# Four z columns of half B computed with half A's bank in a gated recurrence (one core)

## The chip, the cores and the metric

The kernel runs on one core of a Trainium2 chip. A core has TensorE (matrix products into PSUM), VectorE (called DVE in the profile), ScalarE (ACT), GpSimd (POOL) and SyncE (SP, which issues the transfers). Each engine works through its own queue in order; they meet through semaphores, on which an instruction waits. The metric is the device time of one execution in microseconds. Three executions of the kernel before gave 1624.98, 1625.23 and 1625.85 us, and their median is 1625.23 us.

## What is computed

A recurrence over 512 time steps, batch 8, width 512, all in fp32, and a residual:

```python
def step(h, x_t):
    fused = sigmoid(concatenate([x_t, h]) @ w_W + w_b)
    hidden_state, output_state = split(fused, 2)        # r and z
    memory_state = x_t @ wx_W + wx_b + hidden_state * (h @ wh_W + wh_b)
    h_new = output_state * h + (1.0 - output_state) * tanh(memory_state)
    return h_new, h_new
out = x + all h_new                                     # h starts from cond_1024
```

Below r is `hidden_state` and z is `output_state`. The products with x do not depend on the state and can be made ahead. The three products with h (512 x 512 each, for r, z and wh) are on the way from each step to the next.

## The kernel before

**Layout.** The 512 units of the state are four blocks of 128. A block's units 0 to 63 belong to half A, units 64 to 127 to half B. A product has 32 rows of batch (four steps of 8, of which one step's are live) and is written to one of four row strips of a PSUM bank, strip `j` (rows 32j to 32j+31) for block `j`. The sum over the 512 old units is split into four chunks `k`: chunks 0 and 1 come from half A of the old state, 2 and 3 from half B. So "A0" is the products of chunk 0 into bank A, four strips side by side, and fp32 makes two passes of each.

**Banks.** Three banks take the products of a step, in two sets that alternate from group to group of four steps (`banks`, line 215). Bank A (256 columns) holds half B's part of wh for chunks 0 and 1, then half A's wh, z and r. Bank D (128 columns) holds half B's z and r. Bank H (64 columns) holds half B's wh for chunks 2 and 3. Before a group begins ScalarE copies the group's x products, with the biases, into the banks (`spread`, line 310, from `xs`); the columns of x for the memory state go through VectorE (`turn_x`). `XP` (line 73) says which columns of `xs` go where.

**Order of a step.** `tc.manual_schedule()` (line 213) keeps the order of each queue as it is written. TensorE takes A0 A1 A2 A3 D0 D1 D2 D3 H2 H3 (`ORDER`, line 27) and then some pieces of the x products (`deal`, lines 555 to 558): three pieces in most steps, four in each sixteenth. In the last 17 steps no x products are left. A2 and A3 leave out bank A's first 64 columns. A0 and A1 need the new half A of the state, A2 and A3 its half B.

After the products VectorE transposes 32 x 32 blocks, because gates and state live with units on partitions. The steps of the element work stand in lines 656 to 688, in this order:

- `turn_r(0)`, `turn_h(0)`, `turn_r(1)`, `turn_z()`: half A's r, wh and z out of bank A (L585, L594, L577), each followed by its sigmoid on ScalarE (line 285 is the helper that records all of ScalarE's activations).
- `memory(0, 0)`: for chunk 0 a scan on VectorE (L565) forms r times wh plus x, and a tanh on ScalarE follows.
- `turn_part()` (L638): half B's part of wh out of bank A. It is the last read of bank A in a step.
- `memory(0, 1)`: the same scan and tanh for chunk 1.
- `turn_r_b()` (L577 and two sigmoids): half B's r out of bank D. Behind them on ScalarE stands `sz`, the sigmoid of half B's 64 z columns, taken straight from bank D.
- `update(0, 0)`, `turn_h(1)` (L594 out of bank H), `update(0, 1)`: the scans that write half A's new state, with bank H's transpose between them.
- `memory(1, 0)`, `memory(1, 1)`: half B's scans and tanhs.
- `turn_sz` (L631): half B's z, after its sigmoid, is transposed from `sz`.
- `update(1, 0)`, `update(1, 1)`: half B's new state.

Small memsets of a tile `idle` stand at some places (`settle`, `turn_sz`); they take a wait ahead of the instruction behind them. `act` (line 284) also removes a dependence between two activations that write the same place. All other waits are set by the framework from what each instruction reads and writes.

Of the kernel before, what the change touches and what calls it, by code (L numbers as in the profile page):

```python
# [7 lines left out]
F32 = mybir.dt.float32  # L8
BF16 = mybir.dt.bfloat16
AF = mybir.ActivationFunctionType  # L10
# [3 lines left out]
P = 128  # L14
NQ = 4
GS = 4
B = 8
HU = 64
# [9 lines left out]

FIRST = "A0 A1 x A2 x x A3 H0 H1 H2 H3 x D0 D1 D2 D3"

BANKS = {"A": 256, "D": 128, "H": 64}

HALF = 192

# [35 lines left out]

SC = slice(128, 512)

XP = {"A": slice(0, 256), "X": slice(256, 384), "D": slice(384, 512), "H": slice(512, 576)}


@with_exitstack
def tile_cond_rnn_residual(
# [43 lines left out]
    const = ctx.enter_context(tc.tile_pool(name="const", bufs=1))  # L121
    xin_p = ctx.enter_context(tc.tile_pool(name="xin", bufs=4))
    out_p = ctx.enter_context(tc.tile_pool(name="outp", bufs=3))
    work = ctx.enter_context(tc.tile_pool(name="work", bufs=4))
# [11 lines left out]
    def load_x(c, half=slice(0, 2), ks=slice(0, NQ)):  # L136

        if c < NCH:
            if c not in xins:
                xins[c] = xin_p.tile([P, 2, NQ, TC * B // 2], F32, tag="xin", name=f"xin_{c}")  # L140
            nc.sync.dma_start(
                out=xins[c][:, half, ks],
                in_=x[c].rearrange("p (e k n) -> p e k n", e=2, k=NQ)[:, half, ks],
            )
# [13 lines left out]
        if k == 0:  # L158
            load_x(0, 1)

    wa = const.tile([P, NQ, NQ, 256], F32, name="wa")
    for k in range(NQ):
        nc.sync.dma_start(out=wa[:, k], in_=wa_d[k])
        if k == 0:
            load_x(1, slice(0, 1))
    wd = const.tile([P, NQ, NQ, 128], F32, name="wd")
    nc.sync.dma_start(out=wd[:, :3], in_=wd_d)
    nc.sync.dma_start(out=wd[:, 3], in_=wd3_d)
    load_x(1, slice(1, 2))
# [38 lines left out]
    def state(hf, i, slot=2):  # L208

        s = i % GS  # L210
        return hT[hf][i % NH][:, B * s : B * s + B, :, slot]

    ctx.enter_context(tc.manual_schedule())
    whole = [{n: psum.tile([P, 512], F32, name=f"{n}{q}") for n in BANKS} for q in range(2)]
    banks = [{n: whole[q][n][:, :w] for n, w in BANKS.items()} for q in range(2)]
    xps = [psum.tile([P, 512], F32, name=f"xp{q}") for q in range(2)]

    def mm(out_, lhsT, rhs, start=False):
        nc.tensor.matmul(  # L219
            out_, lhsT, rhs, start=start, stop=False, skip_group_check=True  # L220
        )
# [62 lines left out]
    def act(key, out_, in_, func, **kw):  # L284
        inst = nc.scalar.activation(out_, in_, func, **kw).ins  # L285
        if key in written:
            tc.declare_no_dep(inst, written[key], reason="ordered through VectorE")
        written[key] = inst
        return inst
# [12 lines left out]
    def keep(g):  # L302

        nc.scalar.copy(xs[g % GS][:, SC], bank_of(g)[:, COLS])

    def source(g, c0, c1):

        return xs[g % GS][:, c0:c1] if g else xps[0][:, c0 - 64 : c1 - 64]

    def spread(g, names):  # L310

        for n in names:
            skip = 64 if n == "A" and not g else 0
            nc.scalar.copy(banks[g % 2][n][:, skip:], source(g, XP[n].start + skip, XP[n].stop))

    def turn_x(g, e):

        c0 = XP["X"].start + 32 * e
        nc.vector.transpose(md1[e // 2][g % 2][:, :, e % 2, 1 + e // 2], source(g, c0, c0 + 32))
# [10 lines left out]
    def inner_weight(n, p, j=slice(0, 2)):  # L330

        a, b = [
            (block(p, 0, 1, j), block(p, 0, 0, j)),
            (block(p, 1, 1, j), ti[:, p, 0, j]),
            (block(p, 1, 1, j), block(p, 0, 1, j)),
            (block(p, 1, 0, j), ti[:, p, 1, j]),
        ][n]
        nc.vector.tensor_tensor(ti[:, p, n, j], a, b, ALU.subtract)
# [113 lines left out]
    def take(it, n=None):  # L452
        while n is None or n > 0:
            if next(it, it) is it:
                return
            n = None if n is None else n - 1

    def x_side():
        for c in range(2, NCH):
            yield from products(c)  # L460
# [9 lines left out]
    later = x_side()  # L470
# [53 lines left out]
    for i in range(T):  # L524
        g, s = divmod(i, GS)
        c, t = divmod(i, TC)
        ps = banks[g % 2]
# [7 lines left out]
        for n in (ORDER if i else FIRST).split():  # L535
            if n == "x":
                take(first[1], 1)
                if k_ == 0:
                    keep(2)
                k_ += 1  # L540
                continue
            bank, k = n[0], int(n[1])
            hs = hT[k // 2][i % NH][:, :, k % 2, 2]
            to, w_ = {
                "A": (ps["A"], wa) if k < 2 else (ps["A"][:, 64:], wa[:, :, :, 64:]),
                "D": (ps["D"], wd),
                "H": (ps["H"], wa[:, :, :, :64]),
            }[bank]
            if bank == "A" and i == 0:
                to, w_ = xps[0][:, :HALF], wa[:, :, :, 64:]  # L550
            for j in range(NQ):
                mm(to[32 * j : 32 * j + 32, :], hs, w_[:, k, j])
        if i == 0:
# [9 lines left out]
        def scan(c_, out_, d0, d1):  # L563

            return nc.vector.tensor_tensor_scan(  # L565
                *[t_[:, :, c_].rearrange("p n c s -> p (n c s)") for t_ in (out_, d0, d1)],
                0.0,
                ALU.mult,
                ALU.add,
            ).ins  # L570

        pa = ps["A"][:, HU:] if i else xps[0][:, :HALF]
        raw = {"h": (pa[:, :HU], ps["H"]), "z": (pa[:, HU : 2 * HU],), "r": (pa[:, 2 * HU :], ps["D"][:, HU:])}

        def turned(n, hf):
            t_ = work.tile([P, 2, 32], F32, tag=f"t{n}{hf}", name=f"t{n}{hf}_{i}")
            inst = nc.vector.transpose(t_.rearrange("p c n -> p (c n)"), raw[n][hf]).ins  # L577
            return t_[:, :, rows], inst
# [5 lines left out]
        def turn_r(q):  # L584
            nc.vector.transpose(tr[:, q], raw["r"][0][:, 32 * q : 32 * q + 32])  # L585
            act(
                ("r", 0, q, g % 2, s),
                md0[0][g % 2][:, rows, q : q + 1, 1].rearrange("p n c -> p c n"),
                tr[:, q : q + 1, rows],
                AF.Sigmoid,  # L590
            )

        def turn_h(hf):
            inst = nc.vector.transpose(  # L594
                md1[hf][g % 2][:, :, :, hf].rearrange("p n c -> p c n"), raw["h"][hf]
            ).ins
            h_done[hf] = inst
            if hf == 0 and i + 1 - NH in pool_done:
                tc.add_manual_dep(inst, pool_done[i + 1 - NH].name, SYNC)
# [16 lines left out]
        def turn_r_b():  # L616
            t_, _ = turned("r", 1)
            for q in range(2):
                act(
                    ("r", 1, q, g % 2, s),  # L620
                    md0[1][g % 2][:, rows, q : q + 1, 2].rearrange("p n c -> p c n"),
                    t_[:, q : q + 1],
                    AF.Sigmoid,
                )
            sz = work.tile([P, HU], F32, tag="sz", name=f"sz_{i}")
            act(("sz", i % 4), sz, ps["D"][:, :HU], AF.Sigmoid, scale=-1.0)
            return sz

        def turn_sz(sz):
            done = [  # L630
                nc.vector.transpose(hd0[1][i % 2][:, :, q, 2], sz[:, 32 * q : 32 * q + 32]).ins  # L631
                for q in range(2)
            ]
            mark = nc.vector.memset(idle[:, IDLE - 3 : IDLE - 2], 0.0).ins
            tc.add_manual_dep(mark, done[0].name, SYNC)

        def turn_part():
            nc.vector.transpose(md1[1][g % 2][:, :, :, 0].rearrange("p n c -> p c n"), ps["A"][:, :HU])  # L638
# [6 lines left out]
        def memory(hf, q):  # L645

            c_ = slice(q, q + 1)
            scan(c_, ms[hf], md0[hf][g % 2][:, rows], md1[hf][g % 2][:, rows])
            act(("n", hf, q, i % NH), state(hf, i, 1)[:, :, c_], ms[hf][:, :, c_, 1 + hf], AF.Tanh)

        def update(hf, q):
            new = hT[hf][(i + 1) % NH][:, B * s1 : B * s1 + B]
            z_ = hd0[hf][i % 2][:, rows] if hf else hd0[hf][i % 2]
            return scan(slice(q, q + 1), new, z_, hT[hf][i % NH][:, rows])

        turn_r(0)
        turn_h(0)
        turn_r(1)
# [1 line left out]
        memory(0, 0)  # L660
        if i:
            turn_part()
        memory(0, 1)
        if i == 0:
            for p in (3, 4):
                inner_weight(0, p)
        sz = turn_r_b()
        update(0, 0)
        turn_h(1)
        update(0, 1)  # L670
# [5 lines left out]
        if i == T - 1:  # L676
# [4 lines left out]
                ALU.add,  # L681
            )
        memory(1, 1)
        turn_sz(sz)
        update(1, 0)
        update(1, 1)
        for hf in range(2):
# [130 lines left out]
```

## Time and profile before

| | us |
|---|---|
| median of three runs | 1625.23 |
| the profiled execution | 1626.4 |
| its span (first to last instruction) | 1624.6 |
| TensorE busy | 1613.8 (99%) |
| weight loads busy | 1311.1 (81%) |
| VectorE busy | 1414.4 (87%) |
| ScalarE busy | 1092.7 (67%) |
| GpSimd busy | 539.7 (33%) |

The durations come from one profiled execution, 1.2 us above the median. In the profile PE stands for TensorE's products, and PEld for its weight loads, which run beside the products; `hT` is the state, `md0` and `md1` feed the scans for the memory state, `hd0` holds z for the scans that write the new state, `tr` and `tz` are transposed products, `m` is the memory state, `xp` the banks of the x products. A row of the time line gives start, length, engine, line, operation, tiles (written <- read), shape and count; neighbouring instructions of a kind are merged into one row. In brackets stands how long the engine was idle before it and what ended that. Matmuls are pipelined and their ends are modelled, so a busy share of 99% doesn't say that the products run at their full rate: the starts of the sets of products do.

### The profile page before, as it was taken

How to read it: one execution, taken by the hardware profiler on the slowest of the kernel's cores; microseconds unless marked ns; L12 is line 12 of the kernel's file. 1: busy time of each engine (PE TensorE's matmuls, PEld its weight loads, DVE VectorE, ACT ScalarE, POOL GpSimd, SP SyncE). 2: the span in 40 equal slices, each digit the busy share in tenths (PEclk: the TensorE clock that was granted, in tenths of full speed). 3: DMA queues.
4: the chain of work that ended last, by engine and by line, in shares of the span. 5: the costliest groups of instructions: out<-in, count | busy, mean ns of one | idle time of the engine just before them, and what ended most of it. 6: DMA issues, size and time to landing. Idle time of an engine off the chain costs nothing.

```text
span 1624.6 us, 121051 instructions
## 1 busy us (share of the span) xinstructions
PE 1613.8 (99%) x49211; PEld 1311.1 (81%) x49211; DVE 1414.4 (87%) x12269; ACT 1092.7 (67%) x6545; POOL 539.7 (33%) x1443
## 2 busy tenths in 40 slices
PE   9999999999999999999999999999999999999998
PEld 6888888888888888888888888888888888888876
DVE  8988888888888888888888888888888888888887
ACT  4766666666666666666666666666666666666666
POOL 2223333333333333333333333333333333333321
PEclk9999999999999999999999999999999999999999
DMA  5011111111111111111111111111111111111110
GB/s 192 12 40 33 29 37 38 43 32 31 33 42 40 35 33 32 39 39 38 35 29 37 38 43 32 30 34 42 40 34 35 31 39 38 38 35 24 31 35 10
DMA packets 66225, 62.10 MB, mean 38 GB/s; under 512 B 9856, under 2 KB 64000, under 8 KB 65664
## 3 DMA queue, kind: packets, MB, share of 16 engines
q1 hardware_dynamic: 65664, 54.35, 12.8%
q8 instruction: 385, 6.31, 1.6%
q14 instruction: 176, 1.44, 0.3%
HBM read 14.96 MB, written 8.39 MB: 14 GB/s over the span
## 4 chain that ended last, share of the span: by engine, by line
PE 98%; DVE 1%; DMA 0%; issue 0%; SPq 0%; ACT 0%
PE A L219 49%; PE D L219 27%; PE xp L219 16%; PE H L219 7%; DMA wx<-in_wx_dram 0%; DVE tr L585 0%; DVE md1B L638 0%; DVE tr L577 0%; DVE md1A L594 0%; DVE tz L577 0%; DVE hT L565 0%; DVE m L565 0%; SPq L132 0%; ACT hT L285 0%; DVE hd0B L631 0%
## 5 line engine op out<-in xcount | busy, mean ns | idle before, releaser
L219 PE MATMUL A<-wa,hT 128*32 128x256 f32 x16352 | 875.8, 354 | 3.8 <-DVE hT L565 3.8
L219 PEld LDWEIGHTS A<-wa,hT 128*32 128x32 f32 x16352 | 500.5, 123 | 256.5 <-DVE hT L565 132.9
L219 PE MATMUL D<-wd,hT 128*32 128x128 f32 x16384 | 541.1, 273 | 0.0
L219 PEld LDWEIGHTS D<-wd,hT 128*32 128x32 f32 x16384 | 480.7, 122 | 21.4 <-issue 0.3
L734 POOL TENSOR_TENSOR ot<-xin,hT 128x32 f32<-128x32 f32 x503 | 135.1, 269 | 1043.1 <-DVE hT L565 1025.5
L285 ACT ACTIVATE md0A<-tr 128x8 f32<-128x8 f32 x1024 | 215.7, 211 | 375.9 <-DVE tr L585 366.9
L285 ACT ACTIVATE hT<-m 128x8 f32<-128x8 f32 x2048 | 380.7, 210 | 46.1 <-DVE m L565 0.2
L585 DVE STREAM_TRANSPOSE tr<-A 128x32 f32<-128x32 f32 x1022 | 199.6, 195 | 198.8 <-PE A L219 197.8
L285 ACT ACTIVATE hT<-hT 128x16 f32<-128x16 f32 x1024 | 232.1, 227 | 92.5 <-DVE hT L565 91.1
L219 PE MATMUL H<-wa,hT 128*32 128x64 f32 x8208 | 208.4, 219 | 0.0
L219 PEld LDWEIGHTS H<-wa,hT 128*32 128x32 f32 x8208 | 185.8, 122 | 0.0
L565 DVE TENSOR_TENSOR_SCAN hT<-hd0B,hT 128x24 f32<-128x24 f32 x1024 | 172.0, 208 | 1.4 <-DVE hT L565 1.4
L565 DVE TENSOR_TENSOR_SCAN m<-md0A,md1A 128x16 f32<-128x16 f32 x1024 | 172.0, 168 | 0.0
L565 DVE TENSOR_TENSOR_SCAN hT<-hd0A,hT 128x24 f32<-128x24 f32 x1024 | 169.5, 166 | 0.0
L285 ACT ACTIVATE md0B<-tr 128x8 f32<-128x8 f32 x1024 | 159.9, 206 | 1.1 <-DVE tr L577 1.1
L565 DVE TENSOR_TENSOR_SCAN m<-md0B,md1B 128x24 f32<-128x24 f32 x1024 | 154.5, 192 | 0.0
L631 DVE STREAM_TRANSPOSE hd0B<-sz 128x32 f32<-128x32 f32 x1024 | 148.9, 190 | 0.0
L219 PE MATMUL xp<-ti,si 128*32 128x192 f32 (+1 forms) x3120 | 146.8, 295 | 0.0
L450 POOL TENSOR_TENSOR xs<-ff 128x192 f32<-128x192 f32 x240 | 139.8, 599 | 0.1
L638 DVE STREAM_TRANSPOSE md1B<-A 128x64 f32<-128x64 f32 x511 | 133.1, 260 | 0.0
L577 DVE STREAM_TRANSPOSE tr<-D 128x64 f32<-128x64 f32 x512 | 127.8, 250 | 0.1
L594 DVE STREAM_TRANSPOSE md1B<-H 128x64 f32<-128x64 f32 x512 | 127.3, 249 | 0.0
(110 smaller groups left out, 1855.6 us busy)
## 6 DMA issues: line engine op xcount, KB each, us to landing
ff<-tt SPq DMA_DIRECT2D x120, 96.0 KB, 2.4
ff<-tt SPq DMA_DIRECT2D x120, 72.0 KB, 2.5
out_dram<-ot SPq DMA_DIRECT2D x128, 64.0 KB, 1.8
xin<-in_x_dram SPq DMA_DIRECT2D x112, 64.0 KB, 2.1
ff<-ff SPq DMA_DIRECT2D x60, 96.0 KB, 2.1
ff<-ff SPq DMA_DIRECT2D x60, 72.0 KB, 2.7
wx<-in_wx_dram SPq DMA_DIRECT2D x4, 768.0 KB, 8.3
wa<-in_wa_dram SPq DMA_DIRECT2D x4, 512.0 KB, 10.6
```

What stands on the lines that cost most here:

```text
L219: nc.tensor.matmul(out_, lhsT, rhs, start=start, stop=False, skip_group_check=True)
L285: inst = nc.scalar.activation(out_, in_, func, **kw).ins
L450: nc.gpsimd.tensor_tensor(to, a, b, ALU.add)
L565: return nc.vector.tensor_tensor_scan(*[t_[:, :, c_].rearrange("p n c s -> p (n c s)") for t_ in (out_, d0, d1)], 0.0, ALU.mult, ALU.add,).ins
L577: inst = nc.vector.transpose(t_.rearrange("p c n -> p (c n)"), raw[n][hf]).ins
L585: nc.vector.transpose(tr[:, q], raw["r"][0][:, 32 * q : 32 * q + 32])
L594: inst = nc.vector.transpose(md1[hf][g % 2][:, :, :, hf].rearrange("p n c -> p c n"), raw["h"][hf]).ins
L631: nc.vector.transpose(hd0[1][i % 2][:, :, q, 2], sz[:, 32 * q : 32 * q + 32]).ins
L638: nc.vector.transpose(md1[1][g % 2][:, :, :, 0].rearrange("p n c -> p c n"), ps["A"][:, :HU])
L734: pool_done[i + 1] = nc.gpsimd.tensor_tensor(ot[:, t], x_of(c, slice(0, NQ), t, 1), hTs[(i + 1) % NH][:, :, :, B * s1 : B * s1 + B, 2].rea ...
```

## The change

Four of half B's z columns (units 64 to 67 of each block) leave bank D and are appended to bank A. Bank A becomes 260 columns wide (196 in A2 and A3), bank D 124. The weights `wa` and `wd`, the biases, the x columns and the copies into the banks follow. The sigmoid `sz` is split in two: the 60 later columns stay where they were, behind half B's r. The four early ones are read from bank A by an activation of their own, which stands on ScalarE behind the tanh of `memory(0, 0)` and ahead of that of `memory(0, 1)`; in the program's order it follows `turn_part`. Both write one tile `sz`, which is transposed as before.

```diff
+EARLY = 4
+
-BANKS = {"A": 256, "D": 128, "H": 64}
+BANKS = {"A": 256 + EARLY, "D": 128 - EARLY, "H": 64}
...
-XP = {"A": slice(0, 256), "X": slice(256, 384), "D": slice(384, 512), "H": slice(512, 576)}
+XP = {
+    "A": slice(0, 256 + EARLY),
+    "X": slice(256 + EARLY, 384 + EARLY),
+    "D": slice(384 + EARLY, 512),
+    "H": slice(512, 576),
+}
...
-    wa = const.tile([P, NQ, NQ, 256], F32, name="wa")
+    wa = const.tile([P, NQ, NQ, BANKS["A"]], F32, name="wa")
...
-    wd = const.tile([P, NQ, NQ, 128], F32, name="wd")
+    wd = const.tile([P, NQ, NQ, BANKS["D"]], F32, name="wd")
...
-                to, w_ = xps[0][:, :HALF], wa[:, :, :, 64:]
+                to, w_ = xps[0][:, : HALF + EARLY], wa[:, :, :, 64:]
...
-        pa = ps["A"][:, HU:] if i else xps[0][:, :HALF]
-        raw = {"h": (pa[:, :HU], ps["H"]), "z": (pa[:, HU : 2 * HU],), "r": (pa[:, 2 * HU :], ps["D"][:, HU:])}
+        pa = ps["A"][:, HU:] if i else xps[0][:, : HALF + EARLY]
+        raw = {
+            "h": (pa[:, :HU], ps["H"]),
+            "z": (pa[:, HU : 2 * HU],),
+            "r": (pa[:, 2 * HU : 3 * HU], ps["D"][:, HU - EARLY :]),
+        }
...
-            sz = work.tile([P, HU], F32, tag="sz", name=f"sz_{i}")
-            act(("sz", i % 4), sz, ps["D"][:, :HU], AF.Sigmoid, scale=-1.0)
-            return sz
-
-        def turn_sz(sz):
+            act(("sz", i % 4), sz[:, EARLY:], ps["D"][:, : HU - EARLY], AF.Sigmoid, scale=-1.0)
+
+        def turn_sz():
...
+        sz = work.tile([P, HU], F32, tag="sz", name=f"sz_{i}")
         turn_r(0)
...
         memory(0, 0)
         if i:
             turn_part()
+        act(("sz early", i % 4), sz[:, :EARLY], pa[:, 3 * HU :], AF.Sigmoid, scale=-1.0)
         memory(0, 1)
...
-        sz = turn_r_b()
+        turn_r_b()
...
-        turn_sz(sz)
+        turn_sz()
```

On the host the columns of the weights and biases are put in the new order (`early` is units 64 to 67 of a block, `later` units 68 to 127):

```diff
+    early, later = slice(64, 64 + EARLY), slice(64 + EARLY, 128)
...
-    wa_d = chunks(cat((whm, half_b), (whm, half_a), (z[D:], half_a), (r[D:], half_a)))
-    wd = units(cat((z[D:], half_b), (r[D:], half_b)))
+    wa_d = chunks(cat((whm, half_b), (whm, half_a), (z[D:], half_a), (r[D:], half_a), (z[D:], early)))
+    wd = units(cat((z[D:], later), (r[D:], half_b)))
```

More of the change, by code (lines that the diff above doesn't have):

```diff
@@ L785, in chunks @@
         return c_(units(a).swapaxes(0, 1))
-    wx_d = chunks(cat((z[:D], half_a), (r[:D], half_a), (wxm, both), (z[:D], half_b), (r[:D], half_b)))
-    wa_d = chunks(cat((whm, half_b), (whm, half_a), (z[D:], half_a), (r[D:], half_a)))
-    wd = units(cat((z[D:], half_b), (r[D:], half_b)))
+    wx_d = chunks(
+        cat((z[:D], half_a), (r[:D], half_a), (z[:D], early), (wxm, both), (z[:D], later), (r[:D], half_b))
+    )
+    wa_d = chunks(cat((whm, half_b), (whm, half_a), (z[D:], half_a), (r[D:], half_a), (z[D:], early)))
+    wd = units(cat((z[D:], later), (r[D:], half_b)))
     wd_d, wd3_d = c_(wd[:, :3]), c_(wd[:, 3])
@@ L792 @@
     bias_d = (
-        cat((whb, half_a), (zb, half_a), (rb, half_a), (wxb, both), (zb, half_b), (rb, half_b), (whb, half_b))[0]
+        cat(
+            (whb, half_a),
+            (zb, half_a),
+            (rb, half_a),
+            (zb, early),
+            (wxb, both),
+            (zb, later),
+            (rb, half_b),
+            (whb, half_b),
+        )[0]
     )
```

## The prediction

> **What bounds it now.** I read the cores' spans first, then the chain that ended last, then one step of the time line, then the last steps. The clock was never throttled:
>
> ```profile
> core 0: 1624.6 us, clock 1.000
> ```
>
> In the chain every piece of a step in the middle of the run is TensorE's (start us, length us, what):
>
> ```profile
> 799.84 1.52 PE A L219 x32
> 801.37 0.87 PE D L219 x32
> 802.24 0.22 PE H L219 x16
> 802.46 0.49 PE xp L219 x16
> 802.95 1.53 PE A L219 x32
> ```
>
> A step takes 802.95 - 799.84 = 3.11 us. Bank D's products stream 4 x 128 columns in 0.87 us, 1.70 ns for a column of all four row strips. Bank A's 2 x 256 + 2 x 192 = 896 columns would take 1.523 at that rate; the row shows 1.53 at its widest. So TensorE alone needs about 3.10 us, and some 0.01 us of a step is lost inside bank A. Where? The same step, all engines:
>
> ```profile
> 801.18 1.06 PE L219 MATMUL D<-wd,hT 128*32 128x128 f32 x32
> 801.43 0.22 DVE L585 STREAM_TRANSPOSE tr<-A 128x32 f32<-128x32 f32 x1 [0.50 <-PE A L219]
> ...
> 802.04 0.26 DVE L638 STREAM_TRANSPOSE md1B<-A 128x64 f32<-128x64 f32 x1
> ...
> 802.16 0.43 ACT L285 ACTIVATE hT<-m 128x8 f32<-128x8 f32 x2
> 802.20 0.15 DVE L565 TENSOR_TENSOR_SCAN m<-md0A,md1A 128x16 f32<-128x16 f32 x1
> ...
> 802.31 0.25 DVE L577 STREAM_TRANSPOSE tr<-D 128x64 f32<-128x64 f32 x1
> 802.48 0.17 DVE L565 TENSOR_TENSOR_SCAN hT<-hd0A,hT 128x24 f32<-128x24 f32 x1
> ...
> 802.59 0.31 ACT L285 ACTIVATE md0B<-tr 128x8 f32<-128x8 f32 x2
> ...
> 802.77 1.71 PE L219 MATMUL A<-wa,hT 128*32 128x256 f32 x32
> ...
> 802.86 0.20 DVE L565 TENSOR_TENSOR_SCAN m<-md0B,md1B 128x24 f32<-128x24 f32 x1
> ...
> 803.09 0.32 ACT L285 ACTIVATE hT<-m 128x8 f32<-128x8 f32 x2
> ...
> 803.34 0.33 DVE L565 TENSOR_TENSOR_SCAN hT<-hd0B,hT 128x24 f32<-128x24 f32 x2
> ...
> 803.60 0.51 PEld L219 LDWEIGHTS A<-wa,hT 128*32 128x32 f32 x16 [0.26 <-DVE hT L565]
> ...
> 804.30 1.06 PE L219 MATMUL D<-wd,hT 128*32 128x128 f32 x32
> ```
>
> There are two loops. Half A: bank A ends, half A's scans (802.48) give A0 and A1 their weights for 802.77. Half B: bank D ends, is transposed (802.31), takes sigmoid (802.59), scan (802.86), tanh (803.09) and scan (803.34), and A2's weights load at 803.60. A0 and A1 end at 802.77 + 512 x 1.70 ns = 803.64, and a load stands about 0.04 us ahead of its product (estimate from the last steps, below). So A2 is ready a hair late: this is the lost 0.01 us. TensorE and half B's loop are nearly level.
>
> Does half B's loop start with bank D, or with VectorE's queue? Bank D's last products end 0.87 us after bank A's, by the chain; VectorE's first read of A starts at 801.43, and 801.43 + 0.87 = 802.30, where the read of D starts (802.31). VectorE itself would have been free some 0.04 us earlier: where a transpose follows a scan at once, it starts about 0.07 before the scan's end, and this scan ends at 802.35. So the start follows bank D.
>
> In the last steps, which have no x products, TensorE itself waits:
>
> ```profile
> 1571.32 0.62 PEld L219 LDWEIGHTS A<-wa,hT 128*32 128x32 f32 x16 [0.39 <-DVE hT L565]
> 1571.32 1.77 PE L219 MATMUL A<-wa,hT 128*32 128x256 f32 x32 [0.24 <-DVE hT L565]
> ...
> 1572.91 1.06 PE L219 MATMUL D<-wd,hT 128*32 128x128 f32 x32
> ...
> 1574.42 0.44 PE L219 MATMUL A<-wa,hT 128*32 128x256 f32 x4 [0.24 <-DVE hT L565]
> ```
>
> They take 3.10 us all the same: half B's loop. From A's first load to D's first product are 1.59 us against 1.53 in the middle (802.77 to 804.30). Of the 0.06, I give 0.04 to the time from a load to its product and the rest to half B.
>
> **The change, part by part.** *Columns.* Bank A gains 4 columns in each of four k, bank D loses as many: 16 x 1.70 = 27 ns added, 27 removed. No product is added. TensorE's own need stays 3.10 us. That 260, 196 and 124 columns run at the same rate is not shown (every width in the trace is a multiple of 32); between exact and rounded up to the next 8 (A +32 columns, D +0, 54 ns a step) I take exact, because the widths 64, 128 and 896 all give 1.70 to 1.72.
>
> *Half B's loop.* Bank D ends 27 ns earlier after bank A, and its transpose can follow (VectorE is free 40 ns earlier). A2 and A3 get 14 ns longer. The loop loses 13 ns and meets TensorE's 3.10: worth at most the lost 0.01 us in each of some 490 steps, 5 to 7 us.
>
> *Half A's loop.* It loses cover: D is 27 ns shorter, so A0 is due at 802.743 instead of 802.77. Its scan also moves 27 ns forward, being queued behind the transpose of D: end 802.65 becomes 802.62.
>
> *The small sigmoid on ScalarE.* 128 x 4, once a step. The nearest rows are the 64-column sigmoid of D (0.20) and the 8-column ones:
>
> ```profile
> L285 ACT ACTIVATE md0A<-tr 128x8 f32<-128x8 f32 x1024 | 215.7, 211 | 375.9 <-DVE tr L585 366.9
> ...
> L285 ACT ACTIVATE sz<-D 128x64 f32<-128x64 f32 x512 | 104.4, 204 | 0.0
> ```
>
> ```profile
> 16.54 0.32 ACT L314 COPY A<-xp 128x192 f32<-128x192 f32 x1
> ...
> 16.89 0.32 DVE L319 STREAM_TRANSPOSE md1A<-xp 128x32 f32<-128x32 f32 x2 [0.69 <-ACT A L314]
> ```
>
> I take 0.15 to 0.21 us, and 0.06 to 0.11 until the next can start (a pair of some 0.21 each takes 0.31 at the least, at 802.59). When does it start? The last two rows show the program holding VectorE's read of a PSUM bank until ScalarE's read of the same bank ends (16.86, then 16.89), though neither writes there. So the sigmoid must wait for the transpose L638 that ends at 802.30 and, in an instruction of its own, for TensorE. Half A's second tanh, queued behind it, goes from 802.38 (the pair at 802.16 ends at 802.59, less 0.21) to about 802.42 to 802.50. Behind that tanh wait the second half-A scan and bank D's sigmoids (due 27 ns earlier than before, at 802.565, and 0.10 to 0.12 behind the tanh): between nothing and 0.05 us late. I take 0.01 us, as most of the interval meets the due time. The 64-column sigmoid becomes 60 wide: nothing.
>
> The Trainium skill, page "ScalarE: Activation LUTs", section "What ACT_TABLE_LOAD costs", gives an activation with immediates 186 ns + 0.833 ns a column, with 93 ns of overlap; its 239 ns for 64 columns is not what the trace shows (204). By the page the small one takes 189 ns and blocks for about 96, which stays inside what I allow.
>
> *A0's wait.* Bank A now has a reader on ScalarE. The next step's A0, which writes the bank, must wait for VectorE (weights) and for ScalarE. The sigmoid itself is done by about 802.6, no matter. But a second wait is a second instruction: the queues of VectorE and ScalarE show such waiting instructions of their own (515 and 128), and TensorE shows once what one costs when it ends last. Only one state tile is cleared by GpSimd, that of step 7, so there A2's load waits for two engines:
>
> ```profile
> L565 DVEq EVENT_SEMAPHORE  x515: 21/21/21, 23.0 to 1621.7; - x172
> ```
>
> ```profile
> L285 ACTq EVENT_SEMAPHORE  x128: 17/17/17, 36.0 to 1620.9; - x128
> ```
>
> ```profile
> 0.73 0.30 POOL L191 MEMSET hT<- 128x192 f32 x1 [0.29 <-POOLq L802]
> ...
> 43.16 0.21 DVE L565 TENSOR_TENSOR_SCAN hT<-hd0B,hT 128x24 f32<-128x24 f32 x1
> ...
> 43.48 0.17 PEld L219 LDWEIGHTS A<-wa,hT 128*32 128x32 f32 x4
> ...
> 802.70 0.14 PEld L219 LDWEIGHTS A<-wa,hT 128*32 128x32 f32 x4
> ```
>
> With one wait the load starts 0.05 us after the scan's end (802.65, 802.70), and the four strips' loads start within 0.02 (0.14 less one load's 0.12). With two it starts 0.11 after (43.37, 43.48), and the last strip 0.05 after the first. The 43.48 load had an old GpSimd wait beside a fresh VectorE wait, just what A0 gets, with ScalarE's the old one. So A0's first load comes at 802.62 + 0.11 = 802.735 (exact ends), its product at 802.775, 0.03 us after it is due; the last strip lags 0.03 more. Behind A0 stands everything of the step. What queues on TensorE behind A0 is A1 to A3 and D, and VectorE waits for their last strip.
>
> It concerns steps whose bank was read in the step before: three of each group of four (the groups take turns with two sets of banks). From a level start they cost, against 3.113 now (the 3.11 above, a digit finer): the first +19 ns (3.10 + 0.03), the second and third +49 each (the lag of 0.03 is met by VectorE, which sees bank A end that much later, and made anew). The fourth has no double wait: it pays the lag back through half B's loop, 3.10 + 0.03 against 3.113, +17. Together 134 ns in four steps. Every sixteenth step has a fourth x piece, 0.16 us of cover, so one of its +49 is hidden:
>
> ```profile
> 1565.20 1.53 PE A L219 x32
> 1566.72 0.87 PE D L219 x32
> 1567.82 0.65 PE xp L219 x16
> 1568.47 1.56 PE A L219 x32
> ```
>
> Sum: 32 x (4 x 134 - 49) = 15.6 us, with 128 x 0.01 = 1.3 us for ScalarE's delay in the fourth steps: about +16 us. The bounds of A0's wait are nothing (the old wait moves to the extra instruction, and VectorE's stays at the load) and 62 ns a step with the lag. I take the step-7 row, as it is the only one with both waits on TensorE.
>
> The rest I cost at nothing: 512 more ScalarE instructions and copies of 260 and 124 columns in place of 256 and 128 lie beside ScalarE's wait for the next bank A (0.7 us a step, the 366.9 us of the md0A row); uncovered, four columns of a copy are 0.007 us, by the 192 columns in 0.32. Bank A's weights grow by 32 KB and bank D's shrink as much; the transfers lie under the first x products, and uncovered they are 0.2 us, once, at the first slice's rate:
>
> ```profile
> GB/s 192 12 40 33 29 37 38 43 32 31 33 42 40 35 33 32 39 39 38 35 29 37 38 43 32 30 34 42 40 34 35 31 39 38 38 35 24 31 35 10
> ```
>
> No queue of SyncE or GpSimd is touched.
>
> The profiled execution took 1626.4 us, 1.8 over its span of 1624.6; the median of the runs is 1625.23. 1626.4 + 16 = 1642.4, so **1641 us** on the median's scale.
>
> The Trainium skill, page "PSUM — Partial Sum Buffer", section "PSUM bank collisions raise a hardware error", says that two engines must be kept apart on one bank and quadrant, reads against reads included; the pair at 16.89 agrees. By that rule both new waits are needed, and the time is the one above; were reads free, ScalarE's delay alone (1.3 us) would go.
>
> **Rivals.** (a) *A0's double wait costs nothing*, because the late wait stays on the load. For it: A0 had 0.03 us to spare (802.70 + 0.04 against 802.77). Against it: step 7. Then the loop's 13 ns is won: 12 ns x 490 = 5.5 us, **1619.7**, if ScalarE's delay stays under 0.013; this is the case on the other side. Chance 0.20. (b) *The wait comes, but in part*: the lag of the strips or the late load alone. 0 to 19 ns in three steps of four, less 13 in the fourth: **1623 to 1632**, middle 1629. Chance 0.16. (c) *The forecast*, 1634 to 1648. Chance 0.55. (d) *The transpose of D does not move*, VectorE's queue holding it: A0's load is 27 ns later still in some 350 steps, +9 us, **1650**; chance 0.05. (e) *The new widths run rounded up*: 54 ns a step, 27 us, **1652** or more; chance 0.04.
>
> **How the numbers follow.** Forecast 1641. The range 1618 to 1650 takes in (a), (b), (c) with its bounds and the near half of (d); the rest of (d), (e) and the far ends of (a) and (c) stay outside, under 2 in 10. About 0.2% (3.2 us) is what a measurement of this kernel can tell from no change: faster is (a) less 0.01, 0.19; same is 0.07 of (b) and that 0.01, 0.08; slower is 0.09 of (b) with (c), (d) and (e), 0.73.
>
> **What would show it.** Right: in three steps of four A0's first load starts 0.11 us after half A's scan and TensorE shows idle time ahead of A0; the chain passes through VectorE and A0's load; steps of 3.13 to 3.16 us. The transpose of D starts 0.85 us, not 0.88, after VectorE's first read of A. A2's load no longer ends a wait that matters. Wrong: steps of 3.10 us with A0's loads at 0.05 us after the scan (rival a); D's sigmoids over 0.05 us late behind the second tanh would make ScalarE the place instead.

## The result and the profile after

The changed kernel takes 1642.7 us in the median (1641.5 to 1642.9), the kernel before beside it 1625.85 (1625.0 to 1626.4): a ratio of 1.0102 (1.0087 to 1.0117), 16.9 us more. The profiled execution took 1642.7 us too, its span 1640.8, again with the clock at 1.000.

The chain that ended last, in the middle of the run (start us, length us, what):

```profile
801.03 1.59 PE A L226 x32
802.62 0.85 PE D L226 x32
...
804.18 1.54 PE A L226 x32
...
807.28 1.60 PE A L226 x32
```

Bank D takes what it should (0.85 us is the 0.87 of before less 27 ns). The loss lies in bank A: 1.59 and 1.60 us in two of these steps, 1.54 in the one between. Two steps of the time line, the lines of the path alone, the step without loss first:

```profile
802.67 0.22 DVE L596 STREAM_TRANSPOSE tr<-A 128x32 f32<-128x32 f32 x1 [0.62 <-PE A L226]
...
803.41 0.21 ACT L292 ACTIVATE hT<-m 128x8 f32<-128x8 f32 x1
...
803.52 0.25 DVE L588 STREAM_TRANSPOSE tr<-D 128x64 f32<-128x64 f32 x1
...
803.64 0.17 ACT L292 ACTIVATE sz<-A 128x4 f32<-128x4 f32 x1
803.69 0.17 DVE L572 TENSOR_TENSOR_SCAN hT<-hd0A,hT 128x24 f32<-128x24 f32 x1
803.71 0.21 ACT L292 ACTIVATE hT<-m 128x8 f32<-128x8 f32 x1
...
803.91 0.66 PEld L226 LDWEIGHTS A<-wa,hT 128*32 128x32 f32 x16
...
806.40 0.26 DVE L647 STREAM_TRANSPOSE md1B<-A 128x64 f32<-128x64 f32 x1
806.52 0.21 ACT L292 ACTIVATE hT<-m 128x8 f32<-128x8 f32 x1
...
806.78 0.17 ACT L292 ACTIVATE sz<-A 128x4 f32<-128x4 f32 x1
806.81 0.17 DVE L572 TENSOR_TENSOR_SCAN hT<-hd0A,hT 128x24 f32<-128x24 f32 x1
806.85 0.20 ACT L292 ACTIVATE hT<-m 128x8 f32<-128x8 f32 x1
...
807.08 0.21 DVE L572 TENSOR_TENSOR_SCAN hT<-hd0A,hT 128x24 f32<-128x24 f32 x1
807.09 0.65 PEld L226 LDWEIGHTS A<-wa,hT 128*32 128x32 f32 x16 [0.19 <-ACT hT L292]
```

Half A's first scan, which writes A0's weights, ends at 803.69 + 0.17 = 803.86, and A0's load starts at 803.91: 0.05 us. In the next step it ends at 806.98 and the load starts at 807.09: 0.11 us. That the row names ScalarE (`<-ACT hT`) doesn't mean that ScalarE was late: what A0 waits for there is the early sigmoid, and that ended at 806.95 (806.78 + 0.17), before the scan. The profile names the engine of the wait that the load itself holds, and the last thing which that engine had done (here a tanh that A0 does not wait for). VectorE's wait, which ended last, sits in a waiting instruction ahead of the load that the time line does not show. The trace has it: in three steps of four, those whose bank was read by the early sigmoid, an event instruction (one that only waits) on TensorE's queue waits for VectorE, and the load behind it holds ScalarE's semaphore alone (378 of 383 such loads). Over the run these loads stand 0.114 us after the scan (median), the others 0.052.

On ScalarE the extra instructions can be counted (row of events: count, shortest/median/longest, first and last start):

```profile
L292 ACTq EVENT_SEMAPHORE  x637: 17/17/38, 26.0 to 1636.8; - x160
```

There were 128 of them before. The early sigmoid starts at 806.78, 0.12 us after the read of the bank that it must wait for (806.40 + 0.26); in the step before, 0.09 us after it (803.29 + 0.26, 803.64). Here too the trace has VectorE's wait in the extra instruction.

### The profile page after: what moved, and what is told of

The parts are those of the page before. It is cut to its first block, busy times and chain, and to the rows that moved or that the text cites. A ratio compares the mean times of both kernels' runs of the same rounds, so it can differ in the third digit from the quotient of the medians.

```text
span 1640.8 us, 122576 instructions
## 1 busy us (share of the span) xinstructions
PE 1630.6 (99%) x49211; PEld 1399.0 (85%) x49211; DVE 1411.8 (86%) x12269; ACT 1070.3 (65%) x7057; POOL 538.5 (33%) x1443
## 4 chain that ended last, share of the span: by engine, by line
PE 98%; DVE 1%; ACT 0%; issue 0%; ACTq 0%
PE A L226 50%; PE D L226 26%; PE xp L226 16%; PE H L226 7%; DVE tr L596 0%; DVE md1B L647 0%; ACT md0A L292 0%; ACT hT L292 0%; ACT sz L292 0%; DVE md1A L605 0%; DVE tz L588 0%; DVE tr L588 0%; DVE m L572 0%; ACT hd0A L292 0%; DVE hT L572 0%
## 5 line engine op out<-in xcount | busy, mean ns | idle before, releaser
L226 PE MATMUL A<-wa,hT 128*32 128x260 f32 x16352 | 903.5, 359 | 4.8 <-ACT hT L292 2.6
L226 PEld LDWEIGHTS A<-wa,hT 128*32 128x32 f32 x16352 | 562.7, 123 | 213.2 <-DVE hT L572 111.2
L226 PE MATMUL D<-wd,hT 128*32 128x124 f32 x16384 | 538.8, 269 | 0.0
L226 PEld LDWEIGHTS D<-wd,hT 128*32 128x32 f32 x16384 | 489.9, 122 | 7.6 <-issue 0.3
L292 ACT ACTIVATE hT<-m 128x8 f32<-128x8 f32 x2048 | 376.3, 208 | 50.5
L226 PE MATMUL H<-wa,hT 128*32 128x64 f32 x8208 | 219.9, 219 | 0.0
L226 PEld LDWEIGHTS H<-wa,hT 128*32 128x32 f32 x8208 | 195.8, 122 | 0.0
L572 DVE TENSOR_TENSOR_SCAN hT<-hd0A,hT 128x24 f32<-128x24 f32 x1024 | 191.4, 187 | 1.8 <-ACT hT L292 1.8
L292 ACT ACTIVATE md0B<-tr 128x8 f32<-128x8 f32 x1024 | 156.6, 203 | 1.4 <-DVE tr L588 1.1
L226 PE MATMUL xp<-ti,si 128*32 128x192 f32 (+1 forms) x3120 | 152.1, 295 | 0.0
```

The costliest lines, as they stand in the source:

```text
L226: nc.tensor.matmul(out_, lhsT, rhs, start=start, stop=False, skip_group_check=True)
L572: return nc.vector.tensor_tensor_scan(*[t_[:, :, c_].rearrange("p n c s -> p (n c s)") for t_ in (out_, d0, d1)], 0.0, ALU.mult, ALU.add,).ins
```

## The experiments

Seven kernels were run, each beside the kernel before. Three ask which part of the change is the loss, one tries a way round it, and three ask what it is about two waits that costs.

### The wait alone

The kernel before; A0 gets the second wait and nothing else changes.

```diff
-                mm(to[32 * j : 32 * j + 32, :], hs, w_[:, k, j])
+                inst = mm(to[32 * j : 32 * j + 32, :], hs, w_[:, k, j])
+                if s and bank == "A" and k == 0 and j == 0:
+                    tc.add_manual_dep(inst, written["n", 0, 1, (i - 1) % NH].name, SYNC)
```

> The kernel before with its columns and its one 64-column sigmoid; only the first product of A0 is made to wait, in three steps of four, for half A's second tanh of the step before as well (long done by then), so that it waits for two engines. W (the second wait at A0 is the loss): A0's load starts 0.11 us after half A's scan instead of 0.05 and its strips' loads spread, three steps of four take 3.14 to 3.16 us, 1639 to 1645 us. S (the small sigmoid on ScalarE, by delaying the tanh behind it, is the loss) and C (260 and 124 columns cost more than 256 and 128): 1625 to 1627 us, as before.

Measured: 1639.7 us against 1626.2, a ratio of 1.0083 (1.0069 to 1.0097): 13.5 us for a wait that is over before the scan's. One step of its time line:

```profile
804.62 0.43 ACT L285 ACTIVATE hT<-m 128x8 f32<-128x8 f32 x2
...
804.93 0.17 DVE L567 TENSOR_TENSOR_SCAN hT<-hd0A,hT 128x24 f32<-128x24 f32 x1
...
805.22 0.64 PEld L219 LDWEIGHTS A<-wa,hT 128*32 128x32 f32 x16 [0.18 <-ACT hT L285]
```

The tanh that A0 waits for ends at 805.05, the scan at 805.10, the load starts at 805.22: 0.12 us after the scan. So the second wait is not long done, as the expectation has it, but ends only 0.05 us ahead of the scan's. As in the changed kernel the trace has VectorE's wait in the extra instruction and ScalarE's on the load. The second tanh isn't delayed here, nor is any column moved. So the wait by itself makes most of the loss.

### The sigmoid without the columns

The kernel before, with a sigmoid of four of bank A's columns into a spare tile, in the place of the early sigmoid.

```diff
+        spare = work.tile([P, 4], F32, tag="spare", name=f"spare_{i}")
+        act(("spare", i % 4), spare, pa[:, 2 * HU : 2 * HU + 4], AF.Sigmoid, scale=-1.0)
         memory(0, 1)
```

> The kernel before with its columns and its 64-column sigmoid; in the place of the early sigmoid a sigmoid of four of bank A's columns goes into a tile that nothing reads. It gives A0 the two waits and ScalarE the instruction, not the columns. W: 1639 to 1645 us, within 3 us of the run with the wait alone. S: 1639 to 1645 us too, but with the run with the wait alone at 1626. C: 1625 to 1628 us.

Measured: 1642.1 us, 1.0099 (1.0085 to 1.0113), 2.5 us above the wait alone and 0.6 below the change. That is as theory W had it; ScalarE's own delay adds the 2.5: the sigmoids of half B's r start 0.007 us later than with the wait alone (averages of steps 41 to 479 in the two traces).

### The columns without the early sigmoid

The changed kernel, with the sigmoid of half B in one piece, over the first 64 columns of bank D. It leaves out the four early z columns and takes four columns of r in their place.

```diff
-            act(("sz", i % 4), sz[:, EARLY:], ps["D"][:, : HU - EARLY], AF.Sigmoid, scale=-1.0)
+            act(("sz", i % 4), sz, ps["D"][:, :HU], AF.Sigmoid, scale=-1.0)
...
-        act(("sz early", i % 4), sz[:, :EARLY], pa[:, 3 * HU :], AF.Sigmoid, scale=-1.0)
```

> The changed kernel without the early sigmoid: 260 and 124 columns stay, and one sigmoid of the first 64 columns of bank D fills the tile, so four of its columns come from half B's r products in place of the four early z columns. No second wait at A0. W: the loop of half B is 13 ns shorter and nothing is lost, steps of 3.10 us, 1618 to 1622 us. S: the same 1618 to 1622. C: 1630 to 1643 us, with bank A's products over 1.55 us. If half B's loop was not what cost the 0.01 us of a step: 1625 to 1627.

Measured: 1620.1 us, 0.9962 (0.9950 to 0.9975), 6.1 us less than before. Its chain:

```profile
800.05 1.54 PE A L226 x32
801.59 0.85 PE D L226 x32
...
803.15 1.55 PE A L226 x32
...
806.25 1.54 PE A L226 x32
```

Steps of 3.10 us, TensorE's own need. The widths of 260, 196 and 124 columns cost no more than their columns, and half B's shorter loop is worth what the prediction's bound says. Theory C falls. Beside the second wait the columns bring nothing: the change is 0.6 us above the run with the sigmoid alone.

### The wait handed to an x product

The changed kernel; the x products stand behind the early sigmoid in the program, the last piece of each step waits for it, and a one-element copy on ScalarE takes the wait for bank A.

```diff
-        else:
-            deal(later, 4 if (i + LEAD) % TC == TC - 1 else 3)
...
+        if i:
+            take_a = act("seen", seen[:, :1], zeros[:, :1], AF.Copy)
+            tc.add_manual_dep(take_a, a_done.name, SYNC)
...
+        early = act(("sz early", i % 4), sz[:, :EARLY], pa[:, 3 * HU :], AF.Sigmoid, scale=-1.0)
+        if i > PLAIN[-1]:
+            n_mm = len(last_mm)
+            deal(later, 4 if (i + LEAD) % TC == TC - 1 else 3)
+            if len(last_mm) > n_mm:
+                tc.add_manual_dep(last_mm[-4], early.name, SYNC)
```

> The changed kernel with the same columns and both sigmoids, but the wait for the early sigmoid is taken by the last x piece of the step instead of A0 (which then waits for VectorE alone), and a one-element copy on ScalarE, between half A's two r sigmoids, waits for bank A's products, so that the early sigmoid has one wait of its own in three steps of four. Between A0 and this wait stand no other edits. W: steps of 3.10 us, A0's load 0.05 us after the scan, 1618 to 1624 us, faster than both kernels. S: the sigmoid still stands ahead of the tanh: 1635 to 1645 us. C: 1635 to 1645 us. If the last x piece has to wait for the early sigmoid: up to 0.03 us in some steps, 1624 to 1632.

A miss: 1674.4 us, 1.0295 (1.0281 to 1.0309), outside every figure given. From TensorE's row (what its idle time waited for, us, times), and from the chain:

```profile
  ACT sz L295: 62.3, 330
```

```profile
809.64 0.17 ACT sz L295
809.81 0.11 ACT hT L295
809.92 0.03 issue
809.95 0.53 PE xp L229 x8
810.49 1.53 PE A L229 x30
```

The chain leaves TensorE here: it runs through ScalarE, the added copy (0.09 us) among it, and the early sigmoid into the last piece of a step's x products. I had taken that piece to start late in the 0.49 us of x products; it can be two thirds of them (192 of 288 columns), and then it starts before the sigmoid is done. The run says nothing on the theories, only that a wait must not be moved ahead of the time at which it is met. How the 48 us divide between that wait and the copy was not taken apart.

### The same two waits, the other way round

Here the extra instruction is written out: an empty one on TensorE holds the old ScalarE wait, and A0 holds VectorE's. Theory L says that what costs is a late wait in the extra instruction; theory X, that any extra waiting instruction ahead of A0 costs, whatever it waits for.

```diff
+            if n == "A0" and s:
+                tc.add_manual_dep(nc.tensor.nop(nofuse=True).ins, written["sz early", (i - 1) % 4].name, SYNC)
...
+                if bank == "A" and s:
+                    tc.declare_no_dep(inst, written["sz early", (i - 1) % 4], reason="ordered by the wait ahead")
```

On the kernel before, with the wait of the first run (`written["n", 0, 1, (i - 1) % NH]`, the first two lines alone):

> The kernel before with the second wait of the first run (half A's second tanh of the step before, three steps of four), but taken by an empty instruction ahead of A0, so that VectorE's late wait sits on A0's load. L: 1625 to 1627 us, as the kernel before, against 1639.7 with the roles the other way round. X: 1637 to 1642 us.

Measured: 1626.05 us, 1.0000 (0.9991 to 1.0009).

```profile
805.46 0.43 ACT L285 ACTIVATE hT<-m 128x8 f32<-128x8 f32 x2
...
805.77 0.17 DVE L567 TENSOR_TENSOR_SCAN hT<-hd0A,hT 128x24 f32<-128x24 f32 x1
...
806.00 0.22 PEld L219 LDWEIGHTS A<-wa,hT 128*32 128x32 f32 x8
```

0.06 us from the scan's end (805.94) to the load, not 0.12. The same two waits and as many waiting instructions on TensorE's queue (481 in both traces), 13.6 us apart: what costs is the late wait in the extra instruction, and theory X falls. The extra instruction isn't free here either: the load stands 0.11 us after the tanh that it waits for (805.46 + 0.43), in most steps of the run. It costs nothing because that tanh ends 0.05 us before the scan. On the changed kernel:

> The changed kernel, computing the same, with one edit: ahead of A0, in three steps of four, stands an empty instruction on TensorE that waits for the early sigmoid, and A0 itself waits only for VectorE. So there are still two waits and two instructions, but the one that ends last (VectorE's) sits on A0's load, the old one in the extra instruction. L (what costs is that the late wait sits in the extra instruction): A0's load 0.05 us after half A's scan, strips 0.02 apart, steps of 3.10 us, 1619 to 1624 us (1620.1 of the kernel without the early sigmoid, plus 0 to 4 for ScalarE, where the two runs on the kernel before differ by 2.5). X (any extra waiting instruction ahead of A0 costs, whatever it waits for): 1638 to 1645 us.

Measured: 1632.4 us, 1.0039 (1.0025 to 1.0053): 10.3 us of the loss are gone, but it is no 1619 to 1624. One step:

```profile
804.13 0.26 DVE L651 STREAM_TRANSPOSE md1B<-A 128x64 f32<-128x64 f32 x1
...
804.49 0.17 ACT L292 ACTIVATE sz<-A 128x4 f32<-128x4 f32 x1
804.55 0.17 DVE L576 TENSOR_TENSOR_SCAN hT<-hd0A,hT 128x24 f32<-128x24 f32 x1
804.56 0.20 ACT L292 ACTIVATE hT<-m 128x8 f32<-128x8 f32 x1
...
804.78 0.66 PEld L226 LDWEIGHTS A<-wa,hT 128*32 128x32 f32 x16
804.80 0.21 DVE L576 TENSOR_TENSOR_SCAN hT<-hd0A,hT 128x24 f32<-128x24 f32 x1
```

The load is 0.06 us behind the first scan (804.72) in this step, and 0.12 behind the early sigmoid (804.66). It is the sigmoid that it follows: in 349 of the 381 steps with this wait the load stands 0.11 us after the sigmoid's end, which is 0.07 to 0.09 us after the scan (medians of the three steps). So A0's wait is cheaper, not gone. And the second scan ends at 805.01, 0.29 us behind the first; in the kernel without the early sigmoid it is 0.23:

```profile
802.67 0.17 DVE L572 TENSOR_TENSOR_SCAN hT<-hd0A,hT 128x24 f32<-128x24 f32 x1
...
802.90 0.17 DVE L572 TENSOR_TENSOR_SCAN hT<-hd0A,hT 128x24 f32<-128x24 f32 x1
```

The second scan waits for the second tanh, which the early sigmoid holds up. A1's weights come from that scan, but A1's products start hardly later (0.441 us after A0's, 0.439 without the early sigmoid; averages of steps 41 to 479). What counts stands behind the tanh on ScalarE: the sigmoids of half B's r. The transpose of bank D, which feeds them, and these sigmoids, in a step of this kernel and in one of the kernel without the early sigmoid:

```profile
801.25 0.25 DVE L592 STREAM_TRANSPOSE tr<-D 128x64 f32<-128x64 f32 x1
...
801.56 0.30 ACT L292 ACTIVATE md0B<-tr 128x8 f32<-128x8 f32 x2
```

```profile
802.50 0.25 DVE L588 STREAM_TRANSPOSE tr<-D 128x64 f32<-128x64 f32 x1
...
802.78 0.31 ACT L292 ACTIVATE md0B<-tr 128x8 f32<-128x8 f32 x2
```

0.31 us from the one to the other against 0.28; over the run the sigmoids start 0.022 us later on average (counted from bank D's first product) and half B's first new state is written 0.027 later. Of the 0.024 us by which a step is longer, 0.016 lie between A1's first product and A3's (A2 and A3 need half B's state), 0.005 ahead of A0 and 0.003 between A0 and A1. Between these two kernels lie 12.3 us; the kernels before beside them are 0.2 apart. So S wasn't wrong altogether: its delay is there, through half B's loop, but most of it comes to light only where A0's wait is cheaper.

### The same on ScalarE as well

```diff
+        if i:
+            tc.add_manual_dep(nc.scalar.nop(nofuse=True).ins, a_done.name, SYNC)
+        inst = act(("sz early", i % 4), sz[:, :EARLY], pa[:, 3 * HU :], AF.Sigmoid, scale=-1.0)
+        for done in a_all + [copied["A"]] if i else ():
+            tc.declare_no_dep(inst, done, reason="ordered by the wait ahead")
```

`a_all` holds the step's products of bank A, `a_done` the last of them, `copied` the copies into the banks.

> The kernel of the run just described, and the same done on ScalarE: an empty instruction there waits for bank A's products, and the early sigmoid itself only for VectorE's read of the bank (in the first step of a group it keeps a second wait). L: the early sigmoid starts 0.06 to 0.08 us earlier in three steps of four, half A's second tanh with it; 0 to 3 us less than the run just described, 1618 to 1622 us. If ScalarE's delay costs nothing: the same as the run just described within 1 us. X: 1638 to 1645 us.

Measured: 1624.3 us, 0.9987 (0.9979 to 0.9996), 8.1 us less than the run just described and 2.1 less than the kernel before.

```profile
804.74 0.26 DVE L658 STREAM_TRANSPOSE md1B<-A 128x64 f32<-128x64 f32 x1
...
805.03 0.17 ACT L293 ACTIVATE sz<-A 128x4 f32<-128x4 f32 x1
805.11 0.20 ACT L293 ACTIVATE hT<-m 128x8 f32<-128x8 f32 x1
805.15 0.17 DVE L583 TENSOR_TENSOR_SCAN hT<-hd0A,hT 128x24 f32<-128x24 f32 x1
...
805.37 0.22 PEld L226 LDWEIGHTS A<-wa,hT 128*32 128x32 f32 x8
```

The sigmoid starts 0.03 us after the read of the bank (805.00), not 0.10 as in the run before it (804.39 to 804.49), and the load 0.05 after the scan (805.32). The mechanism is the expected one; its size was not: I had given ScalarE 0 to 3 us, and 1624.3 lies above the 1618 to 1622 expected. 4.2 us remain to the kernel without the early sigmoid. The trace shows where most of them are: in the first step of a group VectorE's wait still stands in an extra instruction, the sigmoid starts 0.09 us after the read, and the step from there to the next is 0.02 us longer than without the early sigmoid; the other three are longer by 0.002 to 0.007 (averages of steps 41 to 479).

## Why the prediction was right, and where its sizes were off

1641 us were forecast and 1642.7 measured, inside the 1634 to 1648 of rival (c), the forecast. The sum itself gives 16.9 us, which the prediction carries on as 16; rival (a)'s 12 ns x 490 are 5.9 us, not 5.5.

**TensorE and half B's loop nearly level.** Shown: without the second wait the new columns give steps of 3.10 us and 6.1 us, where the prediction says 5 to 7 us at most.

**The widths** (rival e) and **the transpose of D** (rival d). Bank A takes 1.54 us where nothing waits. The transpose of D starts 0.85 us after VectorE's first read of A (802.67 to 803.52), as forecast. Both rivals are out.

**A0's wait.** The late load, its reason (the late wait in the extra instruction, as at step 7) and the place are as forecast: 0.11 us in the lossy step, 0.05 in the step without a second wait. The wait alone is worth 13.5 us; the working gave 15.6. The steps show why. Bank D's first products, and VectorE's first read of A in the same steps (time line):

```profile
796.10 1.06 PE L226 MATMUL D<-wd,hT 128*32 128x124 f32 x32
799.25 1.06 PE L226 MATMUL D<-wd,hT 128*32 128x124 f32 x32
802.40 1.06 PE L226 MATMUL D<-wd,hT 128*32 128x124 f32 x32
805.54 1.03 PE L226 MATMUL D<-wd,hT 128*32 128x124 f32 x32
808.67 1.06 PE L226 MATMUL D<-wd,hT 128*32 128x124 f32 x32
```

```profile
796.37 0.22 DVE L596 STREAM_TRANSPOSE tr<-A 128x32 f32<-128x32 f32 x1 [0.43 <-PE A L226]
...
805.79 0.22 DVE L596 STREAM_TRANSPOSE tr<-A 128x32 f32<-128x32 f32 x1 [0.42 <-PE A L226]
```

From row to row, in the prediction's count (in which the step without a second wait is the fourth), they take 3.15 and 3.15 us (the second and third), 3.14 (the fourth, up to 805.54) and 3.13 (the first of the next round), 12.57 together; the prediction has 3.16 twice and 3.13 twice (12.586, its 134 ns over 4 x 3.113). First and fourth are right within the rows' digits. The mis-sized term is the lag of the strips in the second and third. The lag itself is as forecast: D's products of a step take 1.06 us with it, 1.03 without (805.54). But VectorE starts 0.27 us after D's first product where the strips lag (796.10) and 0.25 where they don't, so it meets 0.02 of the 0.03 that the prediction passes on.

**ScalarE's delay.** Put at 1.3 us, measured at 2.5 (the sigmoid without the columns against the wait alone). The delay of the second tanh fell into the upper part of its bracket of 0.04 to 0.12 us: 0.30 to 0.33 us after the first tanh in the steps above, against 0.22 before. What the prediction does not see is how much lies under A0's wait: with most of that wait out of the way the early sigmoid costs 12.3 us (1632.4 less 1620.1). The delay goes through the sigmoids of half B's r, as the prediction has it, to the loads of A2 and A3. As long as A0 is late by itself, A2's products are late too, and the delay costs little: in the steps with the second wait alone A2's load stands 0.065 us ahead of its product, in the kernel before 0.028 (medians). The two mis-sized terms go opposite ways, 13.5 + 2.5 = 16.0 for the 15.6 + 1.3 = 16.9 of the prediction's sum; that the forecast came so close is in part luck. Of the 0.9 us between 16.0 and the measured 16.9, 0.3 lie between the kernels before of the two comparisons; the rest was not taken apart.

**Rival (a)**, the double wait at no cost, was the right question with the wrong price. With the roles exchanged the wait does cost nothing (1626.05 on the kernel before). But the changed kernel then stands at 1632.4, not at 1619.7: its condition, ScalarE's delay under 0.013 us, is not met (0.022 us at the sigmoids of half B's r), and the early sigmoid ends too late for A0's load to be quite on time.

**What would show it.** The loads and the steps showed it. The chain did not: it was to pass through VectorE and A0's load, but stays on TensorE's products, as the page's shares say.

```profile
PE 98%; DVE 1%; ACT 0%; issue 0%; ACTq 0%
```

Nor does TensorE show much idle time ahead of A0: 4.8 us in the whole run ahead of all of bank A's products. The ends of products are modelled, and a late product is drawn as a long one before it; so the loss has to be read from bank A's pieces, 1.59 in place of 1.54 us.

## What to carry to other kernels

Before an instruction gets a reader or a writer on another engine, ask which instruction must now wait for two engines, and which of the two waits ends last: an old wait is free only while the late one still sits on the instruction that needs it, and while the old one ends early enough (some 0.06 us before the late one, by the 0.11 and 0.05 us of these loads). If the late one doesn't sit there, put the old wait into an empty instruction ahead, where its time has come, and look again, because the next delay may have been hidden behind the first.

## What the runs showed of the chip that was not expected

- TensorE's load starts 0.05 us after the end of a wait that it holds itself (803.86 to 803.91) and 0.11 to 0.12 us after the end of a wait in the extra instruction ahead of it, whether that is the scan's (805.10 to 805.22), the early sigmoid's (804.66 to 804.78) or the tanh's (805.89 to 806.00). The later of the two decides. On ScalarE the same exchange moved an activation's start from 0.10 to 0.03 us after what it waits for.
- The 4-column sigmoid takes 0.17 us (row at 803.64) and lets the next start after 0.07 (803.71). The Trainium skill, page "ScalarE: Activation LUTs", section "What ACT_TABLE_LOAD costs", would give an estimate of 186 + 4 x 0.833 = 189 ns with 93 of overlap, about 96 until the next: the measurement is shorter on both counts.
